# The second product of a soft mixture of experts, with its output the other way round

## The chip, the core and the metric

The kernel runs on one core of a Trainium2 chip, in one launch. Its time is the device time of an execution in microseconds; the profile is of one execution of its own, and times inside it count from the first instruction of its span. Engines: PE (TensorE, the matrix engine, with PEld for its weight loads), DVE (VectorE), ACT (ScalarE), POOL (GpSimd), and SP, whose queue issues almost all transfers. Everything is in 32-bit floats. The profile records each matmul instruction twice (x32 records are sixteen instructions).

## What is computed

Two batches of 1024 tokens with 256 features pass four layers with residuals: a windowed cross-attention, a grouped feed-forward layer without a nonlinearity, a sigmoid cross-attention, and a soft mixture of experts. The change lies in the last one:

```python
xn = rms_norm(x, gamma_x); se = rms_norm(slot_embeds, gamma_slot)
logits = einsum('bsd,etd->bset', xn, se)             # 1024 tokens x 1024 slots
dispatch = softmax(logits, axis=1)                   # over tokens
slots = einsum('bsd,bset->betd', xn, dispatch)
h = gelu(slots @ w1)                                 # 1024 slots x 1024
processed = h @ w2                                   # 1024 slots x 256
combine = softmax(logits.reshape(b, s, e * t), -1)   # over slots
out = einsum('bnd,bsn->bsd', processed, combine)
x = x + out
```

## The kernel before, in words

The four large products of this layer (slots, hidden, processed, combined) are each computed, for each batch, with seven products of half-size matrices instead of eight. Sums and differences of quarters are formed on DVE or POOL ahead of a product, and products are added up in their PSUM banks or by DVE behind it. With quarters a11, a12, a21, a22 of the left matrix and b11 to b22 of the right one, the products are numbered: p1 is a11 b11, p2 is a12 b21, p5 is a21 (summed) with t1, p6 is a22 or s2 with t2, p4 is a22 with t4, p7 is s3 with b12, and p3 (the product with b22) adds a12 or s4. A bank has 128 partitions x 512 columns; a key ("a", "b", "c", "e", "d0" ...) names it, and `onto(key, ...)` writes the matmuls of one product, into a new bank or on top of one.

The stages stand in the program in this order, for batch 0 and batch 1: logits with their exponentials (`ecs`, weights for combining, divided by a sum per token at the end; `lgs`, weights for dispatch); `gather` (slots); `hidden` (with gelu); `processed`; `combined`. The order of PE, DVE, POOL and SP in this last part is the order in which the Python code issues instructions (a manual schedule), and so is ACT's. To fill PE while sums are made, stages of batch 1 are issued between those of batch 0 by callbacks: `in_processed_0(i)` is called behind product i of processed 0, `in_combined_0(i)` behind product i of combined 0, and so on. `gpsimd_after(element)` makes POOL copy one element of a tile, so that it goes on only when DVE has written that tile.

`processed` makes `prs[b, g]`: slots on partitions, features along the free axis. In `seven`, each of its products is four groups (m) of four matmuls, each with a 128x128 block of the hidden tile as weights and a 128x128 block of w2 as the moving operand (line 777, tiles pp_a, pp_b, pp_c, pp_e). The same helper writes the products of `combined` (pc_a, pc_b, pc_c, pc_e, pc_d), with 128x128 blocks of the exponentials as weights and 128-column blocks of `prs` and its sums as the moving operand. `gather` (psl_a, psl_b, psl_c, psl_e, line 488) and `hidden` (pmh_a, pmh_b, pmh_c, line 627) use moving operands of 512 columns.

The exponentials `ecs[q]` are turned (tokens and slots exchanged) before combining, by `turn(q, h, by)` for token group q and half h: DVE transposes 32x32 squares of a 128x2048 tile (line 335, four instructions), SP writes the tile to DRAM (line 160, `swap_out`), and four transfers read it back with the blocks exchanged (line 165, `swap_in`). The transposes write one of two buffers (seT, or xT in the pool mx). SP issues in order, and a read waits there until its write has landed; whatever stands behind it on SP waits too. For batch 0 the turns stand in hidden 0; for batch 1, `turn_out` of token group 1's two halves in processed 0 (both writes, then all eight reads), those of group 2 and 3 in combined 0 and hidden 1.

`pieces`, `first_sums`, `next_sums` and `last_sums` are the sums of quarters of the turned exponentials; `sum_rights` those of `prs`. `add` puts a combining product, scaled per token by `zrs`, onto the residual; `store` sends a finished 128x256 block to the output, on ACT's queue for the second half of batch 1 and on SP's otherwise.

## Time and profile before

| | |
|---|---|
| runs | 412.05, 413.05, 414.04 us (median 413.05) |
| the profiled execution | 411.93 us |
| its span, first to last instruction | 410.1 us |
| granted clock of PE over the span | 0.999 |
| PE busy | 405.3 us (99%) |
| DVE, ACT, POOL busy | 294.6, 148.0, 118.2 us |
| transfers | 64.05 MB, mean 156 GB/s |

In the lines of groups, the figures behind a bar are the busy time of the group, the mean time of one record in ns, and the idle time of the engine before it with its releaser. In a timeline the columns are start, duration (of all merged records), engine, line, operation and tiles. In the table of stretches there are the length, then for PE, PEld, DVE, ACT and POOL the busy time with the number of records, then the granted clock of PE, the share of the DMA engines' time, and GB/s.

Stages of the part that the change touches, by the starts of PE's groups: processed 0 from 258.4 to 283.4, then gather 1 and combined 0 in turns to 332.4, hidden 1 to 356.5, processed 1 to 381.5, combined 1 to 406.7.

### The profile page before, as it was taken

To read this page: it belongs to the slowest core of one execution; us is meant where nothing else is said; L and a number is where in the kernel's file an instruction comes from. 1 tells how busy PE (TensorE), PEld (TensorE's weight loads), DVE (VectorE), ACT (ScalarE), POOL (GpSimd) and SP (SyncE) were. 2 spreads that over 40 slices of the span, in tenths; PEclk is the share of its full clock that TensorE was granted. 3 is DMA by queue.
4 is the path that set the end of the run, shared out by engine and by line. 5 is a ranking of instruction groups with operands and counts; after the bars stand their busy time and mean duration, and the time that the engine had idled before them with its cause. 6 is when DMAs were issued, how large, how long until landed. Compare 5 with 4: busy or idle time off the path is not lost.

```text
span 410.1 us, 5880 instructions
## 1 busy us (share of the span) xinstructions
PE 405.3 (99%) x2110; PEld 281.6 (69%) x2110; DVE 294.6 (72%) x655; ACT 148.0 (36%) x293; POOL 118.2 (29%) x121
## 2 busy tenths in 40 slices
PE   8999999999999999999999999999999999999996
PEld 7878988888554445444444444898967644599996
DVE  2786888736568688998799887696925797838544
ACT  1145548712455431433671175940110026510100
POOL 2111341311012220253950459083399200000000
PEclk9999999999999999999999999999999999999999
DMA  6999992504523854567000114889060175740003
GB/s 250 418 412 422 395 398 77 229 26 137 161 82 115 231 175 157 132 198 207 6 0 0 53 54 139 212 271 199 2 200 6 32 254 177 205 105 2 2 0 104
DMA packets 27775, 64.05 MB, mean 156 GB/s; under 512 B 6881, under 2 KB 16353, under 8 KB 25057
## 3 DMA queue, kind: packets, MB, share of 16 engines
q1 hardware_dynamic: 27170, 63.15, 47.3%
q10 hardware_dynamic: 576, 0.52, 0.4%
q8 instruction: 17, 0.28, 0.3%
q14 instruction: 12, 0.10, 0.1%
HBM read 45.73 MB, written 17.85 MB: 155 GB/s over the span
## 4 chain that ended last, share of the span: by engine, by line
PE 96%; DVE 1%; POOL 1%; ACT 0%; issue 0%; ACTq 0%
PE pmt L1040 13%; PE pl L287 12%; PE pmh_b L627 5%; PE pq L1395 4%; PE pp_c L777 3%; PE pp_b L777 3%; PE pc_b L777 3%; PE pp_a L777 3%; PE pc_a L777 3%; PE po L1068 3%; PE pf L1409 3%; PE psl_b L488 3%; PE psl_c L488 3%; PE psl_a L488 3%; PE pmh_c L627 3%; PE pmh_a L627 3%
## 5 line engine op out<-in xcount | busy, mean ns | idle before, releaser
L1040 PE MATMUL pmt<-wg 128*128 128x256 f32 x256 | 58.7, 385 | 0.1
L1040 PEld LDWEIGHTS pmt<-wg 128*128 128x128 f32 x256 | 48.7, 193 | 7.8 <-ACT wg L1029 0.5
L424 POOL TENSOR_TENSOR lg<-lg,mb 128x1024 f32<-128x1024 f32 x16 | 37.3, 2367 | 11.2 <-DMA zr<-d_zc 9.7
L316 ACT ACTIVATE ec<-lg,nm 128x1024 f32<-128x1024 f32 x16 | 18.4, 1149 | 37.3 <-DVE nm L295 35.5
L287 PE MATMUL pl<-seT,xhT_late 128*128 128x512 f32 x64 | 28.4, 594 | 0.0
L287 PE MATMUL pl<-seT,xhT 128*128 128x512 f32 x64 | 28.1, 594 | 0.0
L1029 ACT ACTIVATE wg<-wg,less 128x255 f32<-128x255 f32 x56 | 23.3, 495 | 0.1
L1472 ACT ACTIVATE sg<-psg 128x512 f32<-128x512 f32 x32 | 16.5, 602 | 18.2 <-PE psg L1463 18.2
L287 PEld LDWEIGHTS pl<-seT,xhT_late 128*128 128x128 f32 x64 | 12.0, 190 | 14.7 <-issue 14.0
L287 PEld LDWEIGHTS pl<-seT,xhT 128*128 128x128 f32 x64 | 12.1, 190 | 14.3 <-issue 11.5
L335 DVE STREAM_TRANSPOSE tr<-ec 128x512 f32<-128x512 f32 x32 | 19.7, 674 | 0.0
L427 ACT ACTIVATE lg<-lg 128x1024 f32<-128x1024 f32 x16 | 16.2, 1046 | 3.0 <-POOL lg L424 2.9
L500 POOL TENSOR_TENSOR lg<-lg,lg 128x512 f32<-128x512 f32 x12 | 16.8, 1427 | 0.2 <-PE psl_c L488 0.2
L1048 ACT COPY mt<-pmt 128x512 f32<-128x512 f32 x6 | 3.5, 587 | 36.5 <-PE pmt L1040 36.5
L306 DVE TENSOR_TENSOR rmax<-rmax,pl 128x512 f32<-128x512 f32 x24 | 16.3, 679 | 0.0
L1409 PEld LDWEIGHTS pf<-w1s,oT 128*128 128x128 f32 x64 | 11.7, 190 | 6.1 <-DVE oT L1502 1.7
L1409 PE MATMUL pf<-w1s,oT 128*128 128x256 f32 x64 | 15.4, 389 | 0.1
L777 PEld LDWEIGHTS pp_a<-ms,mh 128*128 128x128 f32 x128 | 14.8, 192 | 1.0 <-issue 0.7
L777 PEld LDWEIGHTS pc_a<-pr,ec 128*128 128x128 f32 x128 | 14.8, 192 | 1.0 <-issue 1.0
L627 PE MATMUL pmh_a<-slT,ms 128*128 128x512 f32 x32 | 15.0, 592 | 0.0
L777 PE MATMUL pp_a<-ms,mh 128*128 128x128 f32 x128 | 14.9, 275 | 0.0
L777 PE MATMUL pc_a<-pr,ec 128*128 128x128 f32 x128 | 14.9, 275 | 0.0
(257 smaller groups left out, 848.7 us busy)
## 6 DMA issues: line engine op xcount, KB each, us to landing
wg<-in_wff_dram SPq DMA_DIRECT2D x5, 2052.0 KB, 10.4
d_ec<-tr SPq DMA_DIRECT2D x8, 1024.0 KB, 5.0
ec<-d_ec SPq DMA_DIRECT2D x32, 256.0 KB, 5.6
wg<-in_wff_dram SPq DMA_DIRECT2D x4, 1026.0 KB, 13.6
xT<-in_xT_dram SPq DMA_DIRECT2D x4, 512.0 KB, 14.3
x<-in_x_dram SPq DMA_DIRECT2D x4, 512.0 KB, 16.2
d_a<-tr_a SPq DMA_DIRECT2D x4, 512.0 KB, 3.1
hTa<-d_a SPq DMA_DIRECT2D x16, 128.0 KB, 3.0
```

The lines of the kernel that those rows point to most:

```text
L287: nc.tensor.matmul(pl, lhsT=xhTs[q][:, t, dc, :], rhs=in_order(seT[:, n], dc), start=(dc == 0), stop=(dc == DC - 1),)
L316: nc.scalar.activation(ecs[q][:, :, t, :], lg.rearrange("p (h n) -> p h n", h=2), AF.Exp, bias=nm[:, 1:2], scale=-1.0, accum_out=zcs[b][:, ...
L335: nc.vector.transpose(tr[:, :, :, t, :].rearrange("p r c n -> p c r n"), half[:, t, :].rearrange("p (c r n) -> p c r n", c=EC // 2, r=R4),)
L424: nc.gpsimd.tensor_tensor(lgs[b][s], lgs[b][s], mbs[b], ALU.add)
L488: nc.tensor.matmul(banks[key], lhsT=left[:, k, :], rhs=lg[first + k][:, cols], start=new and k == 0, stop=k == QT - 1, skip_group_check=no ...
L500: add.tensor_tensor(lg[to + k][:, at], lg[x[0] + k][:, x[1]], lg[y[0] + k][:, y[1]], ALU.subtract)
L627: nc.tensor.matmul(to, lhsT=lefts[i][:, ts(j, P)], rhs=rights[b][i], start=first, stop=True, skip_group_check=not first,)
L777: nc.tensor.matmul(banks[key][:, ts(m, P)], lhsT=of(a)(k, m), rhs=w[:, k, :], start=first and m == tiles[0] and k == 0, stop=m == tiles[-1 ...
L1029: nc.scalar.activation(w, w, AF.Identity, bias=less[:, oc : oc + 1])
L1040: nc.tensor.matmul(pm[:, ts(hc, D)], lhsT=w1g[:, oc, ts(hc, P)], rhs=w2g[:, oc, :], start=(oc == 0 and hc == 0), stop=(oc == OC - 1 and hc ...
L1409: nc.tensor.matmul(pf[:, ts(k, D)], lhsT=oTs[q][:, c, ts(2 * i + k, P)], rhs=wo1s[:, c, :], start=(c == 0), stop=(c == C1 - 1),)
L1472: nc.scalar.activation(sg[:, j, :], psgs[j], AF.Tanh, scale=0.5 * DH1**-0.5)
```

## The change

`processed` now writes its result with features on partitions: weights are 128x128 blocks of w2, the moving operand is 512 slots of the hidden tile, and each product is four matmuls instead of sixteen, into one bank. Its quarters c11 to c22 are halves of `prTs[b]` (features x slots). A new step `turn_processed(b, g)` brings each half g back to slots on partitions: two DVE transposes into a buffer with the tag seT, a write of 512 KB to DRAM and four reads of 128 KB, on SP. `combined` reads the turned tile, whose columns of one feature half lie in runs of 32; it hands out its products as functions, which the main code then places one by one.

The order changes with that. In processed 0, group 1's two turns of exponentials stand apart (behind the first and the sixth product) and a pair of sums and POOL's marker move; c12 is copied earlier, by ACT. Then gather 1 starts with p1, t1, p2, p5, and combined 0's q1, q2, q5, q6 are placed between gather 1's products, while q4, q7 and q3 are kept back until behind processed 1. Behind them stand combined 1's products in a new order, r1, r5, r6, r4, r7, r2, r3. In gather 1, p2 has a bank of its own and DVE adds it to p1. Of the four later turns of exponentials, one is in gather 1 and three stand in hidden 1 instead of two. The core of the diff:

```diff
@@ gather
         def p2():
-            onto("a", a12, QT, lo, False)
+            onto("a" if b == 0 else "d", a12, QT, lo, b > 0)

         def c11():
-            nc.scalar.copy(place(b, 0), banks["a"])
+            if b == 0:
+                nc.scalar.copy(place(b, 0), banks["a"])
+            else:
+                nc.vector.tensor_tensor(place(b, 0), banks["d"], place(b, 2), ALU.add)
@@ processed
-        onto = seven(b, "pp", (a11, a12, a21, a22), (b11, b12, b21, b22), left_rows)
+        def onto(key, a, w, first=True):
+            if first:
+                banks[key] = next_bank(f"pp_{b}_{key}")
+            for k in range(QT):
+                nc.tensor.matmul(
+                    banks[key],
+                    lhsT=w[:, k, :],
+                    rhs=a[k // 2][:, k % 2, :],
+                    start=first and k == 0,
+                    stop=k == QT - 1,
+                    skip_group_check=not first,
+                )
+            return banks[key]
...
         sums(a22, a22, s3, SUB)
-        after(4, a22[1][0:1, 1, 511:512])
+        sums(a11, a12, a22, SUB)
+        after(4, a11[1][0:1, 1, 511:512])
         p5 = onto("c", a21, t1)
         nc.scalar.copy(c22, p5)
         p6 = onto("b", a22, t2)
         tt(p6, p6, c11, ADD)
         tt(p5, p6, c22, ADD)
-        sums(a11, a12, a22, SUB)
         after(6)
         p2 = onto("a", a12, b21, False)
         nc.scalar.copy(c11, p2)
-        after(2)
+        nc.scalar.copy(c12, onto("c", a11, b22, False))
+        turn_processed(b, 0)
+        after(3)
         p7 = onto("b", s3, b12, False)
         tt(c22, p7, c22, ADD)
         tt(c21, p7, c21, ADD)
-        after(7)
-        nc.scalar.copy(c12, onto("c", a11, b22, False))
+        turn_processed(b, 1)
+
+    def turn_processed(b, g):
+        if g == 0:
+            tr_prs[b] = const.tile([P, 2, R4, QT, 2, SQ], FP, tag="seT", name=f"tr_pr_{b}")
+        tr = tr_prs[b][:, g]
+        prs[b, g] = keep[b].tile([P, R4, QT, 2, SQ], FP, tag=f"lg_{g}", name=f"pr_{b}_{g}")
+        for d in range(2):
+            nc.vector.transpose(
+                tr[:, :, :, d, :].rearrange("p r c n -> p c r n"),
+                prTs[b][g][:, d, :].rearrange("p (c r n) -> p c r n", c=QT, r=R4),
+            )
+        swap_blocks(
+            tr.rearrange("p r c d n -> p r (c d n)"),
+            prs[b, g].rearrange("p i c d n -> p i (c d n)"),
+            f"pr_{b}_{g}",
+        )
@@ combined: p7 of batch 0 gets a bank of its own
+            if b == 0:
+                p = onto("f", s3, b12)
+                tt(p, p, u2_, ADD)
+            else:
+                p = onto("b", s3, b12, False)
@@ the order
     def in_processed_0(i, element=None):
         if i == 1:
             dispatch(1, 4)
+            turn(1, 0, 0)
         if i == 4:
             gpsimd_after(element)
             for s in range(5, ST):
                 less(1, s)
-            turned = [turn_out(1, h, h) for h in range(2)]
-            for by_row, half in turned:
-                swap_in(by_row, half)
         if i == 6:
             for s in range(5, ST):
                 dispatch(1, s)
             sum_tokens(1, by_tile(aux[1]), by_tile(aux[0]))
+            turn(1, 1, 1)
+        if i == 3:
             pieces(0)
             first_sums(0)

     processed(0, in_processed_0)
     begin_slots(1)
     p1, p2, p3, p4, p5, p6, p7, t1, t2, t3, t4, c11, c21 = gather(1)
+    more_pieces(0)
+    q1, q2, q3, q4, q5, q6, q7, q_first, q_sums, q_later = combined(0)
     p1()
-    combined(0, in_combined_0)
+    t1()
+    p2()
+    c11()
+    p5()
+    last_token_sum(1)
+    t2()
+    turn(2, 0, 1)
+    q_first()
+    q1()
+    p6()
+    next_sums(0)
+    q2()
+    p3()
+    first_sum_of_slots(1)
+    sums_of_slots(1)
+    t3()
     p7()
+    t4()
     p4()
+    q_sums()
+    more_sums(0)
+    q5()
     sum_slots(1, 0)
     c21()
     sum_slots(1, 1)
+    q6()

     def in_hidden_1(j):
-        if j == 1:
+        if j == 0:
             sum_w2(1)
             sum_w2_last(nc.gpsimd)
-            turn(2, 1, 0)
+        if j == 1:
+            turn(3, 0, 0)
         if j == 2:
-            turn(3, 1, 1)
+            turn(2, 1, 1)
+        if j == 3:
+            turn(3, 1, 0)
+
+    def in_processed_1(i, element=None):
+        if i == 4:
             pieces(1)
-        if j == 3:
+            q_later()
+        if i == 6:
             first_sums(1)
-
-    def in_processed_1(i, element=None):
-        if i == 6:
+            last_sums(0)
+        if i == 3:
             next_sums(1)
-            last_sums(1)

     hidden(1, in_hidden_1)
     processed(1, in_processed_1)
-    combined(1, lambda i: None)
+    q4()
+    q7()
+    more_pieces(1)
+    more_sums(1)
+    r1, r2, r3, r4, r5, r6, r7, r_first, r_sums, _ = combined(1)
+    r_first()
+    q3()
+    r1()
+    r_sums()
+    r5()
+    r6()
+    last_sums(1)
+    r4()
+    r7()
+    r2()
+    for t in range(QT):
+        r3((t,))
```

## The prediction

> **What bounds the kernel now.** I read the page first: the busy times and the chain that ended last.

> ```profile
> PE 405.3 (99%) x2110; PEld 281.6 (69%) x2110; DVE 294.6 (72%) x655; ACT 148.0 (36%) x293; POOL 118.2 (29%) x121
> PE 96%; DVE 1%; POOL 1%; ACT 0%; issue 0%; ACTq 0%
> L777 PE MATMUL pp_a<-ms,mh 128*128 128x128 f32 x128 | 14.9, 275 | 0.0
> L488 PE MATMUL psl_a<-lg,xh 128*128 128x512 f32 x32 | 14.4, 593 | 0.0
> ```

> TensorE (PE) works without a gap; its only wait is 1.1 us at the start, and 3.4 us remain after its last matmul (406.67 of 410.1). So a gain has to come out of PE's own pace, and every PE wait that the change makes is added whole. In the two group lines the mean of one (275 and 593 ns) misleads: matmuls overlap. The pace is start to start, which the timeline of PE shows:

> ```profile
> 215.47 3.60 PE L488 MATMUL psl_b<-lg,slT 128*128 128x512 f32 x8
> 218.90 3.60 PE L488 MATMUL psl_a<-lg,xh 128*128 128x512 f32 x8
> 222.33 3.60 PE L488 MATMUL psl_c<-lg,slT 128*128 128x512 f32 x8
> ...
> 258.38 3.73 PE L777 MATMUL pp_a<-ms,mh 128*128 128x128 f32 x32
> 261.95 3.74 PE L777 MATMUL pp_e<-aux,mh 128*128 128x128 f32 x32
> 265.53 3.74 PE L777 MATMUL pp_c<-pr,mh 128*128 128x128 f32 x32
> 269.10 3.74 PE L777 MATMUL pp_b<-m_sums,mh 128*128 128x128 f32 x32
> ```

> One product of four 512-column matmuls takes 3.43 us, one of sixteen 128-column matmuls 3.57 us, for the same multiplications. Then the sync queue (SP), which issues the transfers, in its timeline:

> ```profile
> 249.51 0.38 SPq L160 DMA_DIRECT2D d_ec<-tr  x1
> 253.47 1.73 SPq L165 DMA_DIRECT2D ec<-d_ec  x4
> 255.29 0.38 SPq L160 DMA_DIRECT2D d_ec<-tr  x1
> 263.27 1.73 SPq L165 DMA_DIRECT2D ec<-d_ec  x4
> ...
> 128.55 0.34 SPq L177 DMA_DIRECT2D d_se<-tr_se  x1
> 131.19 1.73 SPq L179 DMA_DIRECT2D seT<-d_se  x4
> ```

> A turn is a write of a 1 MB tile to DRAM and four reads back, which SP holds back until the write has landed. Alone, the write takes 3.96 us (249.51 to 253.47). Issued while the reads of the turn before still run, it lands late: from those reads' issue to the next reads' issue 9.80 us pass (253.47 to 263.27); the later pair, 349.13 to 359.00, has 9.87. A turn of half the size has its write back after 2.64 us (128.55 to 131.19), 1.3 less.

> **The change, part by part.**
> *Processed in 512-slot products.* Removed: 14 products at 3.57 us. Added: 14 at 3.43, taken from the psl rows, which also accumulate four weights into one bank. 14 x 0.14 = 2.0 us less on PE. Nobody else is on that path, so it counts whole; the means (16 x 2 x 275 against 4 x 2 x 593) would promise 4 us a product and are wrong.

> *Combining products.* Still sixteen 128-column matmuls. Their right operand now lies in 32-element runs; the logits' products (L287) read such runs at 429 ns a matmul record, the psl products contiguous ones at 429, so I take 0; by those rows neither gain nor loss is above 0.1 us.

> *Added vector work.* Per batch, four 128x512 transposes (rows of L335: four take 2.48 us). DVE is 72% busy and stands beside PE; sums on runs of 32 I price like L728's 0.68. One more ACT copy position: c11 and c12 (0.59 each) now stand behind the last three exponentials of batch 1, and those behind GpSimd's subtractions, whose marker waits for one more pair of sums. Before, that marker ran at 267.8; now the transposes end at 266.4 and the two pairs (2.35 each) at 271.1. Three subtractions of 2.33 end at 278.3, the last exponential at 279.4, both copies at 280.6, the two transposes at 281.3. The first product that reads those exponentials (p2 of the gather) starts at 285.8 and its fourth matmul at 288.4: covered by 9 us. If that were gone, PE would wait at p2.

> *The first turn of processed, batch 0.* This is where I find a wait. PE starts the seven products at 258.38, as before, and ends them at 282.4; then p1, p2, p5 of the gather (3 x 3.43) bring it to 292.7, where the first combining product q1 needs the four reads of the turned tile. That turn is issued on SP behind two turns of the exponentials (batch 1's halves), which now stand one after the other. The reads at 263.27 are unchanged. The vector transposes of the next turn end at 266.4, so its write is queued behind those reads and its own reads issue at 263.3 + 9.8 = 273.1. The transposes of the turn after that end at 276.3, again while reads run: its reads issue at 282.9. SP reaches the processed tile's write only after that (the tile itself was ready at 281.3): half the size, 9.8 - 1.3 = 8.5, so its reads issue at 291.4. They need the 1.3 us until the fourth issue and 2.6 to 3.4 us to land (d_se), median 3.0: 295.7. PE waits 295.7 - 292.7 = 3.0 us. Bounds: with the fastest landings 2.6 us; with reads that take a microsecond longer in each of the two large turns 5 us. I take 3.0, the sum of medians. The second half (q2) is read back one half turn later: its write 1.3 us behind the first's reads, then 0.5 to issue and 4.3 to land, 302; q2 stands two products behind q1, at 295.7 + 7.0 = 302.7: covered by about 1 us, and every microsecond beyond that is a wait of PE's.

> *GpSimd.* Its four groups of subtractions for the gather (4 x 1.24 each) follow each other from 283; t2's last ends near 295.3 and p6 starts at 299.3, t3's and t4's come by 305.3, before p7 and p4. While GpSimd adds, a DVE pair of 1024 columns takes 4.72 instead of 2.35 (rows at 274.73 and 259.25); the pairs that meet it (first sums, next sums) have 4 us to spare.

> *Order at the end.* Three combining products of batch 0 (10.7 us) stand between processed 1 and its first reader. From the copy of c12 the turn needs 0.8 + 1.2 + 2.6 + 4.3 = 9 us; PE has one 3.43 product and the three kept back, 14.1 us: covered by 5. The thin places are on DVE: r5 needs the first sum of the turned tile, which stands behind the sum on q7's bank, eight additions, a pair of sums and itself (0.8 + 2.2 + 2.35 + 0.7 after a hand-over of 0.2 = 6.2 us), and PE gets there 7.1 us after q7: 0.9 us to spare. q6 has 1.5. Three exponential turns instead of two in the last hidden stage delay no PE operand: hidden 1 starts at 323.7 (295.7 and four products of each kind) instead of 332.4, so the first turn's write issues at 345.3 - 8.7 = 336.6, the reads of the three at 340.5, 350.3 and 360.1, and the last of these land (1.3 + 5.6) at 367, while DVE reaches their sums behind c12's transpose, at 369.7. At the very end the last matmul, one addition and one store follow each other as before.

> *Sum.* -2.0 + 3.0 = +1.0 us. The profiled execution took 411.93 us, span 410.1; that gives 412.9 for it. It lies 1.1 below the median of the runs, 413.05; on that scale 414.1 us.

> **The rivals.**
> *The clock drops in the wait (slower).* Before has no PE idle stretch inside, but it has one behind its last matmul, and the clock in these stretches is:

> ```profile
> 408.00:409.00 1.00, 0.00 (x0) 0.00 (x0) 0.00 (x0) 0.00 (x0) 0.00 (x0) 1.00 0.78 255
> 409.00:409.50 0.50, 0.00 (x0) 0.00 (x0) 0.00 (x0) 0.00 (x0) 0.00 (x0) 0.94 0.00 0
> 409.50:410.10 0.60, 0.00 (x0) 0.00 (x0) 0.00 (x0) 0.00 (x0) 0.00 (x0) 0.50 0.00 0
> ```

> The column before the DMA share is the granted clock: 1.00 until 409, 0.94 over the next half microsecond, then 0.50; so it halved at 409.44, 2.8 us after PE fell idle. A wait of 3.0 us at q1 is just at that point, and decides if it is longer. At the start 14 records of 128 columns took 3.35 us, 239 ns each against 112 later: half pace over at least 3.3 us. The same behind q1 costs up to 3.3 / 2 = 1.7 us: 1.0 + 1.7 = +2.7, 415.8 us. Against it: one instance, at a place where nothing followed. [...]

> *No wait at q1 (faster).* If writes overlap the reads more than at 253 to 263, two steps fall to 8.3 and PE finds its tile: 413.05 - 2.0 = 411.1 us. For it: the writes' packets are few and large. Against: both pairs of before show 9.8 and 9.87.

> *The products do not get cheaper.* Four weights of 128 columns from the small matrix and 512 moving columns should pace like psl; hidden's products, also 512 wide, change bank at each matmul and still pace 0.857 us each, 3.43 for four. If the pace stayed at 3.57, PE would reach q1 7 x 0.14 = 1.0 us later and wait 2.0: sum +2.0, 415.1 us, and up to 416 with the longer landings.

> **How the numbers follow.** About 0.5% (2.1 us) is what a measurement of this kernel can tell from no change. Wait without drop 45%: 413.6 to 414.7. Drop 33%: 415 to 416.3. No wait, or a short one, 15%: 411.0 to 413. Products not cheaper 7%: to 416. Range 411.0 to 416.3. Slower by over 0.5% (above 415.1): the drop, half of the last case and the long end of the wait, 0.41. Faster by over 0.5% (below 411.0): half of the no-wait case, which ends just at that line, 0.09. Within: 0.50.

> **What would show it.** Right: pp products 3.43 us start to start; PE idle once, before the first pc_a of batch 0, about 3 us, released by the reads of pr; three SP rows 273, 283, 291 for the issues of the reads; the clock row there says which of the two cases it is. Wrong: no such idle time, or idle time at q2, r5 or in the last hidden stage, or pp products that keep 3.57.

## The result and the profile after

The changed kernel takes 414.86 us (median of 22 runs, 413.02 to 416.79), the kernel before 412.13 us (22 runs, 411.80 to 416.03): 2.7 us more by the medians, with a ratio of 1.0051 (95% interval 1.0032 to 1.0069). The ratio goes by means, and seven of before's 22 runs (413.05 to 416.03, the rest 411.80 to 412.19) raise its mean, so that the means differ by 2.1 us only; what delays those seven no trace here shows. The three runs of before that the forecast started from, two of these seven among them, had a median of 413.05, 0.9 above that of the 22; this matters below, where the forecast's 414.1 is taken apart.

The page of after: the busy times, the chain that ended last, and the group of the combining products that now has idle time in front of it.

```profile
PE 405.1 (98%) x1774; PEld 254.3 (62%) x1774; DVE 299.1 (72%) x665; ACT 147.4 (36%) x293; POOL 115.7 (28%) x120
PE 89%; DMA 5%; DVE 2%; SPq 1%; POOL 1%; issue 0%; ACT 0%; DVEq 0%; ACTq 0%
L927 PE MATMUL pc_a<-pr,ec 128*128 128x128 f32 x128 | 16.6, 294 | 3.3 <-DMA pr<-d_pr 3.3
```

PE lost 336 records and kept its busy time: 14 products shrank from 32 records to 8 each, and the records do not carry the pace. In the chain a transfer, which had no share before, holds 5%, PE 89% instead of 96%. The last line names the transfer: 3.3 us of idle time ahead of pc_a, released by the reads of `pr`. PE's waits hold nothing else of that size:

```profile
PE pc_a L927 <- DMA pr<-d_pr: 3.3, 1, 3.3
PE busy L96 <- DVE ones L93: 1.1, 1, 1.1
PE pmt L1086 <- DVE wg L1077: 0.2, 1, 0.2
```

(Released thing, releaser; us in total, times, longest.) The second row was there before. The timeline of PE in after, first the new products, then the place of the wait, then the last group:

```profile
258.33 3.60 PE L798 MATMUL pp_a<-mh,ms 128*128 128x512 f32 x8
261.77 3.60 PE L798 MATMUL pp_e<-mh,aux 128*128 128x512 f32 x8
...
289.24 3.60 PE L488 MATMUL psl_c<-lg,aux 128*128 128x512 f32 x8
296.15 5.44 PE L927 MATMUL pc_a<-pr,ec 128*128 128x128 f32 x32 [3.32 <-DMA pr<-d_pr]
301.43 3.60 PE L488 MATMUL psl_b<-lg,aux 128*128 128x512 f32 x8
304.86 3.73 PE L927 MATMUL pc_a<-pr,ec 128*128 128x128 f32 x32
...
406.20 3.74 PE L927 MATMUL pc_d<-pr,ec_s 128*128 128x128 f32 x32
```

The products stand 3.44 us apart (258.33 to 261.77) where they stood 3.57 apart. q1, at 296.15, takes 5.44 us, q2, the same work at 304.86, 3.73: the first ran 1.7 us long. The table of stretches around it gives the reason in the column behind POOL, the granted clock:

```profile
293.00:296.20 3.20, 0.04 (x1) 0.07 (x1) 0.06 (x1) 0.45 (x1) 3.20 (x3) 1.00 0.95 287
296.20:296.60 0.40, 0.40 (x3) 0.40 (x4) 0.40 (x1) 0.00 (x0) 0.40 (x2) 0.76 0.47 184
296.60:299.60 3.00, 3.00 (x16) 3.00 (x16) 0.52 (x1) 0.00 (x0) 3.00 (x3) 0.50 0.18 49
299.60:300.00 0.40, 0.40 (x5) 0.40 (x4) 0.00 (x0) 0.00 (x0) 0.40 (x1) 0.72 0.37 105
300.00:303.00 3.00, 3.00 (x19) 2.19 (x18) 0.00 (x0) 0.59 (x1) 3.00 (x3) 1.00 1.02 357
412.40:413.10 0.70, 0.00 (x0) 0.00 (x0) 0.00 (x0) 0.00 (x0) 0.00 (x0) 0.54 0.00 0
```

PE stands still at full clock, gets its tile, and 0.3 us later the clock halves. A mean of 0.76 over 296.20 to 296.60 puts the fall at 296.41 (0.21 us at full, 0.19 at half), 0.72 over 299.60 to 300.00 the return at 299.82: 3.41 us. The last row has a second fall, behind the last matmul: 0.54 over 0.70 us puts it at 412.46. So the last group starts 3.27 us later than before (406.20 against 402.93): -2.0 for the products, +3.5 for the wait (q1 starts 6.91 us behind the group ahead of it, whose own pace is 3.43; the profile counts 3.3 of it as idle) and +1.7 for the half clock. The 0.2 us wait at the start has no part in it: at 258.33 PE is where it was before. From there to the end of the span before had 7.2 us, after 6.9.

Why the tile is late, in the timeline of SP (after):

```profile
263.49 1.73 SPq L165 DMA_DIRECT2D ec<-d_ec  x4
266.25 0.34 SPq L160 DMA_DIRECT2D d_ec<-tr  x1
273.21 1.96 SPq L165 DMA_DIRECT2D ec<-d_ec  x4
276.26 0.34 SPq L160 DMA_DIRECT2D d_ec<-tr  x1
282.92 1.73 SPq L165 DMA_DIRECT2D ec<-d_ec  x4
284.75 0.37 SPq L160 DMA_DIRECT2D d_pr<-tr_pr  x1
291.64 1.73 SPq L165 DMA_DIRECT2D pr<-d_pr  x4
```

SP reaches the processed tile's write (284.75) only when the reads of the third exponential turn in these rows are issued, and that write lands 6.9 us later, among those reads.

### The profile page after: what moved, and what is told of

Same layout as the page of the kernel before. It is cut to its first block, busy times and chain, and to the rows that moved or that the text cites. A ratio compares the mean times of both kernels' runs of the same rounds, so it can differ in the third digit from the quotient of the medians.

```text
span 413.1 us, 5255 instructions
## 1 busy us (share of the span) xinstructions
PE 405.1 (98%) x1774; PEld 254.3 (62%) x1774; DVE 299.1 (72%) x665; ACT 147.4 (36%) x293; POOL 115.7 (28%) x120
## 4 chain that ended last, share of the span: by engine, by line
PE 89%; DMA 5%; DVE 2%; SPq 1%; POOL 1%; issue 0%; ACT 0%; DVEq 0%; ACTq 0%
PE pl L287 12%; PE pmt L1086 12%; PE pmh_b L630 5%; PE pc_a L927 4%; PE pq L1441 3%; PE po L1114 3%; PE pf L1455 3%; PE psl_b L488 3%; PE pmh_a L630 3%; PE pmh_c L630 3%; PE pc_b L927 3%; PE pp_b L798 2%; PE psl_c L488 2%; PE pp_a L798 2%; PE pp_c L798 2%; PE psg L1509 2%
## 5 line engine op out<-in xcount | busy, mean ns | idle before, releaser
L287 PE MATMUL pl<-seT,xhT_late 128*128 128x512 f32 x64 | 28.4, 594 | 0.0
L287 PE MATMUL pl<-seT,xhT 128*128 128x512 f32 x64 | 28.1, 594 | 0.0
L287 PEld LDWEIGHTS pl<-seT,xhT_late 128*128 128x128 f32 x64 | 12.0, 190 | 14.7 <-issue 14.0
L287 PEld LDWEIGHTS pl<-seT,xhT 128*128 128x128 f32 x64 | 12.1, 190 | 14.3 <-issue 11.5
L927 PE MATMUL pc_a<-pr,ec 128*128 128x128 f32 x128 | 16.6, 294 | 3.3 <-DMA pr<-d_pr 3.3
L335 DVE STREAM_TRANSPOSE tr<-ec 128x512 f32<-128x512 f32 x32 | 19.8, 677 | 0.0
L927 PEld LDWEIGHTS pc_a<-pr,ec 128*128 128x128 f32 x128 | 16.3, 210 | 4.6 <-issue 4.6
L500 POOL TENSOR_TENSOR lg<-lg,lg 128x512 f32<-128x512 f32 x12 | 15.2, 1307 | 0.4 <-PE psl_c L488 0.4
L1441 PE MATMUL pq<-hTa,w1s 128*128 128x512 f32 x32 | 14.8, 605 | 0.0
L1114 PE MATMUL po<-mt,hT_f 128*128 128x256 f32 x64 | 14.6, 382 | 0.1
```

The lines of the kernel that those rows point to most:

```text
L287: nc.tensor.matmul(pl, lhsT=xhTs[q][:, t, dc, :], rhs=in_order(seT[:, n], dc), start=(dc == 0), stop=(dc == DC - 1),)
L335: nc.vector.transpose(tr[:, :, :, t, :].rearrange("p r c n -> p c r n"), half[:, t, :].rearrange("p (c r n) -> p c r n", c=EC // 2, r=R4),)
L927: nc.tensor.matmul(banks[key][:, ts(m, P)], lhsT=v[m // 2][:, m % 2, k, :], rhs=r[:, k], start=first and m == tiles[0] and k == 0, stop=m ...
L1114: nc.tensor.matmul(po[:, ts(t, D)], lhsT=hTfs[q][:, dc, ds(i * GN + t * P, P)], rhs=mts[g][:, dc, :], start=(dc == 0), stop=(dc == DC - 1),)
L1441: nc.tensor.matmul(pq, lhsT=wq1s[:, dc, ts(c, P)], rhs=in_order(hTs[q], dc), start=(dc == 0), stop=(dc == DC - 1),)
```

## The experiments

All are compared with runs of before on the same chip, whose median was 412.0 to 412.1 in each group. The ratios are not those of the medians here either.

**One part alone: only the wider products.** Before, with 512-column products in `processed`, and its result not turned.

```diff
-        onto = seven(b, "pp", (a11, a12, a21, a22), (b11, b12, b21, b22), left_rows)
+        # onto() of the changed kernel, into one bank, returning by_tile(banks[key])
```

> The kernel before with one edit: processed's products are made of four 512-column matmuls, and their result is used as it stands, so it is not turned and the values are not those of the reference. Order, sums, copies and transfers are those of before. Theory (PE's pace start to start): fourteen products at 3.43 instead of 3.57 us, 2.0 us less than before. Rival by the means of one matmul (16 x 2 x 275 ns against 4 x 2 x 593): over 4 us a product less, some 50 us if it counted whole, or bounded by the next engine. Rival (the pace is set by something else than the number of instructions): no difference.

Measured: 410.07 us (409.86 to 411.83), ratio 0.9959 (0.9946 to 0.9973), 2.0 us less. The last group starts at 401.15 instead of 402.93. So the gain that the change aims at is real, and all of it reaches the end.

**The wait taken away: the transposes write straight into the tile that combined reads; the way through DRAM is left out.**

```diff
-        tr = tr_prs[b][:, g]
+        tr = prs[b, g]
-        swap_blocks(...)
```

> The transposes of processed write straight into the tile that combined reads; the write to DRAM and the four reads of each half are left out, so the 32-blocks are not exchanged. Theory (of the whole change only the transfers cost PE time): no PE wait anywhere, clock 1.00, 2.0 us less than before. Rival (the new order has a cost of its own, in banks, ACT or POOL): less than 1.5 us is gained, and PE shows waits that no transfer releases.

Measured: 409.60 us (409.56 to 409.64), ratio 0.9941 (0.9929 to 0.9952), 2.4 us less. PE's waits shrink to the one at the start:

```profile
PE busy L96 <- DVE ones L93: 1.1, 1, 1.1
```

Everything that after loses, 5.3 us against this kernel, hangs on the tile's way through DRAM. Of the 2.4 us the last group's start has 1.9 (401.05); the other 0.4 lie behind it (6.8 us instead of 7.2), in the new order at the end.

**The clock alone: the wait filled with work.** Four 512-column products ahead of q1, into q1's bank, which q1 then overwrites.

```diff
+            if first and key == "a" and b == 0:
+                for _ in range(4):
+                    nc.tensor.matmul(banks[key], lhsT=ident, rhs=m12s[0][:, 0, 0:512],
+                                     start=True, stop=True, skip_group_check=True)
```

> The changed kernel with four more matmuls of 512 columns (4 x 0.857 = 3.43 us) in front of q1, into q1's own bank, which q1 then begins anew: PE works through the time in which it waited, and q1 starts when its reads are there. Theory (the wait costs 3.3 us less 2.0 gained, and the halved clock behind it up to 1.7 us on top in those executions in which it comes): q1 starts at 296.2 as before, the clock stays at 1.00 throughout, no execution takes longer than 413.6 or so: 1.3 us over before, some 1.5 under the changed kernel's median of 414.9. Rival (the clock falls for another reason, or the drop costs nothing): same times and same clock as the changed kernel.

Measured: 413.27 us (413.18 to 413.75), ratio 1.0032 (1.0021 to 1.0043), the clock between 0.999 and 1.000 in all six runs. More work on the critical engine makes after faster by 1.6 us, about what q1 ran long. So the cost of the turn is a wait of about 3.3 and a half clock of 1.7.

**Half of that filling** (`range(2)`).

> After with two 512-column products (of the identity with a tile already there) in the bank of q1 ahead of q1: they take about 1.7 us of the wait of 3.3 us and leave some 1.6 us idle; q1 still starts when its tile has landed, near 296.1. Theory (the clock halves after an idle stretch of around 3 us): no drop, q1's group takes 3.73 us and not 5.44, time as with four such products, 413.3 us, between 413.0 and 413.8. [...]

Measured: 412.84 us (412.41 to 413.66), the clock between 0.999 and 1.000 in all 12 runs: no drop. It is 0.4 us better than the full filling, and below the range I gave: in the profiled runs q1 starts at 295.90 against 296.41, since four products last longer than the wait here. The ratio, 1.0009 (0.9994 to 1.0025), cannot be told from no change; the medians differ by 0.7 us (412.84 against 412.14).

**A quarter** (`range(1)`).

> After with one 512-column product in the bank of q1 ahead of q1 (two of them left 1.2 us idle and the clock full in all executions; none left 3.3 us and most executions had the clock halved). This leaves about 2.1 us. Theory (the clock is decided once per window of 3.41 us, and halves behind a window in which PE was idle for about 2 us or more, so the place of the wait in the window matters): few executions drop, at most one in four, median 412.8 to 413.3, single ones near 414.5. Rival A (a window that holds any idle stretch of 1.7 us, half a window, is enough): about half of the executions or more near 414.5. Rival B (nearly the whole window must be idle): none, as with two products.

Measured: 413.69 us (413.09 to 415.11), ratio 1.0026 (1.0001 to 1.0051). Seven of twelve runs, at 413.1 to 413.8, had no drop (clock 0.999 to 1.000), five, at 414.7 to 415.1, had one (0.995 to 0.996). I had expected an idle stretch of 2.1 us and at most one in four; the stretch was 2.8 us in the profiled run, because the tile landed later (296.7), and that run shows the clock kept over it. The share of drops lies between the theory's and rival A's; rival B, no drop at all, is out. The profiled run's waits, then its table of stretches:

```profile
PE pc_a L933 <- DMA pr<-d_pr: 2.8, 1, 2.8
```

```profile
293.90:295.40 1.50, 0.00 (x0) 0.00 (x0) 0.00 (x0) 0.00 (x0) 1.50 (x2) 1.00 0.94 234
295.50:296.70 1.20, 0.00 (x0) 0.02 (x1) 0.00 (x1) 0.00 (x0) 1.20 (x2) 1.00 1.04 381
296.70:300.00 3.30, 3.29 (x29) 3.30 (x30) 1.84 (x1) 0.00 (x0) 3.30 (x4) 1.00 0.20 61
...
411.40:411.60 0.20, 0.00 (x0) 0.00 (x0) 0.00 (x0) 0.00 (x0) 0.00 (x0) 0.77 0.00 0
```

The last row fixes the phase: a clock of 0.77 over 0.2 us is a fall from 1.0 to 0.5 at 411.51. In after the two falls lie at 296.41 and 412.46, 116.05 us apart, and the half clock between the first fall and its return (299.82) lasts 3.41: 116.05 is 34 times 3.413, so that in after's trace all three changes of the clock lie on a grid of 3.413 us. If the same grid holds in the quarter filling's trace, whose only change is the fall at 411.51, a boundary lies 116.05 us ahead of it, at 295.46, and cuts the idle stretch into 1.6 and 1.2 us; in after the boundaries 293.00 and 296.41 hold 3.15 idle microseconds between them. By these traces what counts is not the length of a stretch but the idle time within one period of the grid: the quarter filling's 2.8 us, 1.6 of them in one period, kept the clock, and 2.5 in one period lost it (after's end, idle from 409.94 to 412.46). The kernel of the next experiment narrows this. Its last group on PE, then two of its stretches behind the last matmul:

```profile
401.71 3.74 PE L927 MATMUL pc_d<-pr,ec_s 128*128 128x128 f32 x32
```

```profile
407.20:407.60 0.40, 0.00 (x0) 0.00 (x0) 0.00 (x0) 0.00 (x0) 0.00 (x0) 0.79 0.00 0
407.50:408.50 1.00, 0.00 (x0) 0.00 (x0) 0.00 (x0) 0.00 (x0) 0.00 (x0) 0.50 0.00 0
```

PE is idle from 405.45, and the clock falls at 407.43 (0.79 over 0.40 us): 2.0 idle microseconds in a period were enough. By these traces the point lies between 1.6 and 2.0, as exactly as the modelled ends of the matmuls allow; half a period (1.7), rival A's figure, lies inside. The shares of runs with a drop agree roughly. As an estimate: if a stretch L falls on the grid by chance and a period needs T idle (T below L, above half of L), the share of drops is (3.41 + L - 2 T) / 3.41. After (L 3.3, 16 of 22 runs with a lowered clock) gives T = 2.1. The quarter filling (2.8, 5 of 12) gives 2.4, but its profiled run is the slowest of the seven without a drop, so the others probably waited less.

**Undo the queue order: turn the second half of group 1's exponentials behind `processed`.** `turn(1, 1, 1)` leaves the callback behind product 6, so that SP takes the processed tile first.

```diff
-            turn(1, 1, 1)          # in in_processed_0, i == 6
     processed(0, in_processed_0)
+    turn(1, 1, 1)
```

> The second turn of group 1's exponentials is issued behind both turns of processed 0 instead of between sixth and seventh product; nothing else moves. Theory (q1 waits because the turned tile's transfers stand behind that turn on SP): the write of the first half issues when its transposes end, near 281.4, alone, lands after 2.6 us, and the reads (1.3 + 3.0) are there at 288.3, before PE reaches q1 at 292.7. The second half is there near 294.5, q2 needs it at 299.7; the moved turn is read back near 303, its sums feed q5 at 313.5. No PE wait, the clock stays at 1.00, and the 512-slot products' 2.0 us remain: 2.0 us less than before, some 4.8 less than the changed kernel's median of 414.9. Rival (the wait only shows at q1 what the vector work, ACT's order and POOL's later start lose): a PE wait of about 3 us stays somewhere near q1, and the time is at least 1 us over before.

Measured: 410.55 us (410.26 to 410.79), ratio 0.9963 (0.9951 to 0.9975). With one line moved, the change is faster than before. SP and PE, each in its timeline:

```profile
280.78 0.34 SPq L160 DMA_DIRECT2D d_pr<-tr_pr  x1
283.88 1.73 SPq L165 DMA_DIRECT2D pr<-d_pr  x4
```

```profile
292.62 3.73 PE L927 MATMUL pc_a<-pr,ec 128*128 128x128 f32 x32
```

The reads issue 7.8 us earlier than in after, q1 starts without a wait and at full clock. Of the 7.8, 4.0 are the write's earlier issue (280.78 against 284.75) and 3.8 its quicker landing (3.1 against 6.9 us): the turn ahead delays the tile by its place in the queue and by its reads in flight, about half each. The tile's transfers on another queue were not tried. The gain is 1.5 and not 2.0, since a new wait stands in hidden 1:

```profile
PE pmh_c L630 <- DVE pr_sums L731: 0.5, 1, 0.5
```

In the timeline of DVE it comes from the row of scales, one per slot (an expectation below calls them per token), which goes out to DRAM (zrow) and comes back as a broadcast (rz):

```profile
317.42 1.29 DVE L606 TENSOR_TENSOR slT<-slT,rz 128x512 f32<-128x512 f32 x2 [2.17 <-DMA rz<-zrow]
```

Its 4 KB write, issued at 310.51, lands 3.3 us later (the broadcast is issued at 313.80): the next exponential turn's reads, issued at 305.98, are in flight.

**The middle place: that turn between the two halves of the processed tile** (behind product 3).

> After with the second exponential turn of batch 1 issued between the turns of the two halves of processed 0. Theory (the wait at q1 is the place in SP's queue alone): the reads of the first half issue near 284 and land near 288, so q1 does not wait; but the second half's write stands behind the large turn, its reads issue near 299.6 and land near 303.9, and q2, which PE reaches at about 299.7, waits some 4 us: about 413 to 414 without a drop of the clock, about 415 to 416 with one. Rival (the sync queue has slack for the second half, or the reads take less behind a large turn): no wait at either, 410.5.

Measured: 416.44 us (415.31 to 418.61), ratio 1.0094 (1.0062 to 1.0125). q1 is free, and the wait sits at q2, as the theory has it. In the profiled run it is 6.4 us long instead of 4, but that run is the slowest of the six (418.61); the two fastest, at a clock of 0.995 and 0.996, took 415.3 and 415.6, within the theory's 415 to 416. PE and the clock in the profiled run:

```profile
PE pc_a L927 <- DMA pr<-d_pr: 6.4, 1, 6.4
```

```profile
303.50:303.90 0.40, 0.00 (x0) 0.00 (x0) 0.40 (x1) 0.00 (x0) 0.40 (x1) 0.98 1.17 195
303.90:304.00 0.10, 0.00 (x0) 0.00 (x0) 0.10 (x1) 0.00 (x0) 0.10 (x1) 0.50 2.41 205
304.00:306.50 2.50, 0.00 (x0) 0.00 (x0) 1.23 (x1) 0.00 (x0) 2.50 (x3) 0.50 0.94 326
...
310.60:310.80 0.20, 0.20 (x3) 0.20 (x3) 0.00 (x0) 0.00 (x0) 0.00 (x0) 0.73 0.55 143
...
416.00:416.80 0.80, 0.00 (x0) 0.00 (x0) 0.00 (x0) 0.00 (x0) 0.00 (x0) 0.83 0.00 0
```

The half-size write takes 8.7 us from its issue (292.74) to the next reads' (301.41), the tile is there at 306.57. The clock is halved for two periods, 303.88 to 310.71 (6.83 us), but only their second part costs time, 2.0 us on q2 (5.78 us instead of 3.73). The last row puts another fall at 416.53, 105.82 us behind the return, 31 times 3.413: the grid of after's trace fits here too.

**The scales on ACT's queue** (with the turn moved as above).

```diff
-        nc.sync.dma_start(out=row, ...)
+        queue = nc.sync if b == 0 else nc.scalar
+        queue.dma_start(out=row, ...)      # and the broadcast back likewise
```

> The version with the turn moved behind processed 0, with batch 1's two small transfers of the per-token scale (a row out and its broadcast back) on ACT's queue. Theory (the 0.5 us wait left there is the row's write behind the exponential turn's reads on SP): the broadcast lands up to 2 us earlier, the wait of hidden 1 for its first sum goes, 409.7 to 410.2 us. Rival (the row's write is late because the DMA engines are busy with the reads, whichever queue issues it): 410.5 us as before the edit.

Measured: 410.45 us (410.11 to 411.02), ratio 0.9938 (0.9914 to 0.9962), by the medians 1.7 us less than before, against 1.5 without the edit; PE's wait in hidden 1 is 0.6. The write is issued at 310.55 and the broadcast at 314.15, no earlier than on SP. The rival holds: on ACT's queue the row takes 3.6 us, on SP's 3.3, so the queue's order does not make it late; without those reads in flight it takes 1.4 us (the version with the next turn moved into hidden 1, below).

**The other buffer for the turns of groups 2 and 3**, so that the first of them need not wait for its buffer (with the turn moved).

> The version with the turn moved behind processed 0, with the four later exponential turns on the other of the two buffers each (group 2's first half no longer waits for the buffer of the turn ahead of it). Theory: its transposes run near 290 instead of 296.3, its write follows the reads ahead of it directly, its own reads issue about 0.8 us earlier, the broadcast of the scales lands that much earlier, and the 0.5 us wait of hidden 1 goes: 409.9 to 410.2 us. Rival (the write in the middle of reads takes as long as before, or the broadcast lands no earlier): 410.5.

Measured: 410.63 us (410.12 to 410.92), ratio 0.9953 (0.9935 to 0.9972). A miss: the write is issued 0.7 us earlier (298.11 against 298.82), and its reads at 305.97 against 305.98. In these two traces the write's end did not move with its issue; that it ends when the reads around it do is inferred, not shown.

**The next turn moved into hidden 1**, so that nothing large is in flight at the scales (with the turn moved).

```diff
-    turn(2, 0, 1)                   # in gather 1
     def in_hidden_1(j):
+        # j == 0..3: turn(2, 0, 0), (3, 0, 1), (2, 1, 0), (3, 1, 1)
```

> The version with the turn moved behind processed 0, with the next exponential turn (group 2, first half) moved out of gather 1 into hidden 1, so that nothing large is in flight when the row of scales is written. Theory: the row lands in some 1.4 us instead of 3.3, the wait of 0.5 us goes, 409.7 to 410.2 us, if four turns fit into hidden 1 (last reads issued near 366, first used behind 369). Rival (the fourth turn comes late): a wait of up to 3 us in combined 1 or at the sums before it, 411 to 413 us.

Measured: 414.98 us (413.32 to 416.48), ratio 1.0053 (1.0033 to 1.0073). The row does land in 1.4 us, and the 0.5 us wait is gone, but a larger one came, at a place neither theory named. PE's waits, then DVE's timeline:

```profile
PE pmh_b L630 <- DVE mh L679: 3.5, 1, 3.5
```

```profile
344.62 2.49 DVE L335 STREAM_TRANSPOSE tr<-ec 128x512 f32<-128x512 f32 x4 [3.54 <-DMA d_ec<-tr]
347.03 0.65 DVE L679 TENSOR_TENSOR mh<-pmh_b,mh 128x512 f32<-128x512 f32 x1
```

The fourth turn's transposes wait for the second turn's write to free their buffer, and a sum that PE needs stands behind them on DVE. The clock drops again in most runs (9 of 12).

**That fourth turn moved behind processed 1's first product.**

> The version with group 2's first turn moved into hidden 1, its fourth turn (group 3, second half) now behind processed 1's first product. Theory (the 3.5 us wait of the version without this step is VectorE's: the fourth turn's transposes stand ahead of a sum of hidden 1 and wait for the buffer until the second turn's write has landed at 344.6): the wait goes, and with it the half clock, 409.9 to 410.4 us; the fourth turn's reads issue no later than before (364), since its write stands behind the third's reads anyway. Rival (the sum that needs those reads now comes first): VectorE waits there for 1 us or more and the last products with it, 411 to 412 us.

Measured: 410.18 us (409.93 to 410.48), ratio 0.9951 (0.9939 to 0.9964), the lowest median of the complete versions. PE's waits:

```profile
PE busy L96 <- DVE ones L93: 1.1, 1, 1.1
PE pmt L1086 <- DVE wg L1077: 0.2, 1, 0.2
```

The fourth turn's reads issue at 363.87, against 364.07 before the move: SP was the limit, not DVE. DVE does wait 1.7 us for them at 371.6, where the rival put a wait, but PE has room there.

**The first three of the four turns one step earlier** instead, the fourth in its old place.

> The version with four later turns, group 2's first turn standing between the last gather sums and hidden 1 and the other three in hidden 1 one step earlier (the fourth in its old place). Theory: the first write issues near 327.5 instead of 330.9, so the buffer is free near 341, when VectorE reaches the fourth turn; no wait in hidden 1 but up to 0.3 us at its first sums, which now stand behind 2.5 us of transposes: 409.9 to 410.4 us. Rival (the transposes ahead of hidden 1's first sums hold up its banks): a wait of 1 to 2 us there, 411 to 412 us.

Measured: 410.67 us (410.25 to 410.87), ratio 0.9960 (0.9946 to 0.9973). Between theory and rival: the fourth turn is no longer in the way, but the first one's 2.5 us of transposes (at 324.66) put VectorE back: those of the turn behind hidden 1's first step start at 329.85 instead of 328.38 (in the version with the next turn moved into hidden 1), and PE waits 0.8 us for the sum behind them (pmh_b at 332.95).

## Why the prediction was right, and where not

*The gain.* Right: the pace fell to 3.43 us, and the wider products alone gave 2.0 us.

*The first turn of processed.* Right in place, cause and size. The three issues of reads were put at 273.1, 282.9 and 291.4 and came at 273.21, 282.92 and 291.64; the wait of 3.0 was 3.3. That moving one turn on SP's queue removes it shows this turn to be the cause, not only the profile's account of it. The sum had both of its effects, the later issue and the slow write among its reads.

*Likeliest case against rival.* Here the choice failed. The forecast took the wait without the drop; that came in 6 of 22 runs. In the other 16 the clock fell, the first rival, and the median is the rival's: its sum, +1.0 + 1.7 = +2.7 us, is what the medians differ by (414.86 - 412.13). The forecast's 414.1 stands near the result because two errors offset each other, 1.7 us for the drop and 0.9 us for a starting point that three runs had put too high. The rival's own range, 415 to 416.3, carries the same 0.9, and the median lies just below it. The profiled run, forecast at 412.9, took 414.89. The price was right (q1 ran 1.7 us long), the point of decision was the weak step. The 45% for the wait without the drop, against 33%, supposed that a wait of 3.0 leaves the clock alone more often than not. No run shows that: the clock fell in 16 of after's 22 runs, before's own row (idle since 406.67, fall at 409.44, 2.8 us later) already spoke against it, and in the run with the moved turn 2.0 idle microseconds in one period of the grid were enough. With T at 2.0 the formula above gives, as an estimate, a drop in seven runs of ten for a wait of 3.0 and in eight for one of 3.3.

*No wait at q1; products not cheaper.* Neither happened. The sums of chances are off here: half of 15% is 0.075 and not 0.09, that case was given a range that begins at 411.0, the line below which the half was put, and the wait without a drop, with a range up to 414.7, has no long end above 415.1. The later turns confirm that writes amid reads are slow: 9.7 us in after from 263.49 to 273.21 and from 273.21 to 282.92.

*The covers.* Right: q2, q6, r5 and the sums of the last hidden stage show no wait in after. q2's margin cannot be read there, since the drop delayed PE as well; the quarter filling, without a drop, had no wait at q2 either.

*The very end.* "As before" missed by 0.3 us: 6.9 us from the last group to the end instead of 7.2. The other order at the end gains a little by itself, also without the way through DRAM (6.8).

*Open.* In five runs of after (415.9 to 416.8 us) the mean clock is 0.992, as if two periods were halved. The trace of the middle place shows two halved periods in a row, but behind 6.4 us of idling; and none of the five was profiled. Two periods with at least 1.6 idle microseconds each need a stretch of 3.2, so 3.3 would give two only if the point lay at the low end, and seldom; a longer wait in those runs, or a second one, would do it too.

## What to carry to other kernels

A tile that went through DRAM cost here what stood ahead of it on its queue (4.0 us) and what was in flight beside it (3.8 us): put the one that the critical engine needs next first, and the bulk that has slack behind it; here one moved line turned +2.7 us into -1.5. Price a wait of the matrix engine together with the clock behind it: a wait of 2.8 or 3.3 us cost up to 1.7 us more in part of the runs, and a few products of no use in the gap won that back. A transfer that is moved for one reader's sake is also a buffer and a place on the vector engine, so look at what its transposes now stand in front of; here that was a sum that PE waited 3.5 us for.
